# Graph kernel on one core: a second, panel-ordered copy of the transposed adjacency for the panel and search loads

## The chip, the cores and the metric

The kernel runs on one core of a Trainium2 chip. The metric is the device time of one execution in microseconds, as a median of several runs. The profile is of one execution, taken by the hardware profiler. A core has the engines PE (matmul, with its weight loads PEld), DVE, ACT, POOL (GpSimd) and SP, which issues transfers; 16 DMA engines serve the core.

## The reference

Four layers follow each other; each adds to x what it computes from x and one sparse 4096 x 4096 adjacency matrix, and normalizes. N is 4096, D is 256.

```
x = LN(x + adj @ (x * W0))                                    # layer 0
R = (adj + I) / rowsum;  Xf = Xa = x;  Z = 0                  # layer 1
for n in (0, 1):
    A  = top_p_attention(Xa, W1, W2, W3)                      # softmax, smallest set holding 0.9, renormalized
    Xf = R @ Xf;  Xa = A @ Xa
    Z  = Z + Xf @ U1[n].T + Xa @ U2[n].T
x = LN(x + LN(x + Z))
s = x @ Hv                                                    # layer 2: softmax over neighbours
x = LN(x + softmax over j with adj[i,j] != 0 of (adj[i,j] * s[j]) @ x)
edge[i] = sum_j adj[i,j] * adj[j,i]                           # layer 3
x = LN(x + concat(x, adj @ x, edge) @ weight + bias)
```

The density of adj falls with the row and column number: the first tiles of 128 nodes have many neighbours, the last ones few.

## The kernel before

Nodes are cut into 32 tiles of P = 128. The adjacency comes in as `pair`, of shape [4096, 32, 2, 128]: for node j and column tile b, 128 numbers of adj[j] and, right behind them, the same 128 columns of the transposed matrix. Each piece of 128 numbers is 512 bytes, so a load of the transposed part alone reads 512 contiguous bytes at a time. The view `adjT_v` (line 188) names the transposed parts by partition p, row tile t, column tile b.

Two kinds of load read that view, both issued on SP's queue.

- A *panel* (JC = 4 row tiles of one column tile, 256 KB) in `adj_matmul` (line 195) and `all_columns` (line 1392). Eight panels make one target tile I, and 32 matmuls (line 205) add up its row of adj @ x. Panels have a pool of five buffers in layer 0 (`loads=5`) and of four in layers 2 and 3.
- A *half* (HB = 8 blocks of 128 x 128, 512 KB) in `find_columns` (line 472), which only looks for nonzeros. It has two buffers.

In layer 0, a target tile is handled densely or by a list. The first 16 tiles are dense (`dense_0`); the last 16 are listed (`listed_0`): for each of them and each class of source nodes, GpSimd gathers only the rows that have a neighbour in the tile. For that, `seen[p, J, b]` must first hold the largest absolute value of row p of row tile J in column tile b. For the dense tiles it is filled by a reduction of each panel on DVE (line 197); for the others, b from 16 to 31, by `find_columns`, with a reduction of each half (line 473). Between the panels of the first five dense tiles stand all 64 halves: seven row tiles J for each target tile, two halves for each J.

When they are done, `list_columns(1)` builds on DVE and PE the lists of sources for the listed tiles, and writes the index tables idx_x and idx_a (line 357). `gather` (line 380) is GpSimd's indirect transfer with such an index; `pack` gathers adjacency pairs of a listed tile (reading `pair`, both parts) and stores the transposed part as `packed`, blocks of [128, up to 5, 128] in DRAM, which later layers read back as pc (line 418). `listed_steps` gathers the feature rows and multiplies (line 434). `out_0` ends a target tile: layer norm on DVE, projections on PE, stores.

Layer 1 (lines 970 to 1330) computes attention of every node against all, narrowed to candidates, with R through the lists; it reads no panel. In layer 2 the first six target tiles use `all_columns` (48 panels), in layer 3 the first three use `adj_matmul` (24 panels); the others use packed blocks and gathered rows. A fallback, `with_all_columns`, is skipped unless a test of the data fails; it uses panels too.

The order of work on each engine is planned by the tile framework when the kernel is built; only two stretches of layer 1 have an order written out by hand (`manual_schedule`) for PE, ACT, DVE and GpSimd. So in layer 0, panels of later dense tiles stand between the halves of earlier ones.

Of the kernel before, what the change touches and what calls it, by code (L numbers as in the profile page):

```python
# [15 lines left out]
OP = mybir.AluOpType  # L16
AX = mybir.AxisListType

P = 128
# [3 lines left out]
NT = N // P  # L23
# [23 lines left out]
HB = 8  # L47
# [12 lines left out]
LE = P // NL  # L60
# [5 lines left out]
JC = 4  # L66


@with_exitstack
def gnn_kernel(ctx: ExitStack, tc: tile.TileContext, x, pair, W0, W1, W2T, W3T, U1T, U2T,  # L70
               ln_g, ln_b, Hv, W3L, b3, out):
    nc = tc.nc
    PSUM = bass.MemoryType.PSUM
# [50 lines left out]
    for j in range(NT):  # L124
        t = big.tile([P, D + 1], F32, name=f"xw_{j}", tag=f"xa{j}", padded_shape=[P, D + 2])
# [59 lines left out]

    adjT_v = pair.rearrange("(t p) b s i -> p t b s i", p=P)
    pair_r = pair.rearrange("j b s i -> (j b) (s i)")

    def adj_matmul(ps, rhs, I, seen=None, width=D, beside=None, stop=True):

        for c in range(NT // JC):
            a = pools["loads"].tile([P, JC, P], F32, name="panel", tag="panel")
            nc.sync.dma_start(a, adjT_v[:, c * JC:(c + 1) * JC, I, 1])
            if seen is not None:
                nc.vector.tensor_reduce(seen[:, c * JC:(c + 1) * JC, I], a, AX.X, OP.max, apply_absolute_value=True)
            if beside is not None:
                beside(c)
            if callable(rhs):  # L200
                b = rhs(c)
            for k in range(JC):
                j = c * JC + k
                r = b[:, k, :] if callable(rhs) else rhs[j][:, :width]
                nc.tensor.matmul(ps[:, :width], a[:, k, :], r, start=(j == 0), stop=stop and j == NT - 1)  # L205
# [97 lines left out]
    seen = const.tile([P, NT, NT], BF16, name="seen")  # L303
# [163 lines left out]

    def find_columns(J):

        for b in range(LE, NT, HB):  # L470
            t = pools["loads"].tile([P, HB, P], F32, name="half", bufs=2)
            nc.sync.dma_start(t, adjT_v[:, J, b:b + HB, 1])
            nc.vector.tensor_reduce(seen[:, J, b:b + HB], t, AX.X, OP.max, apply_absolute_value=True)

    def out_0(I, ps, sums, xin):
        nc.vector.tensor_scalar_add(rone[:, I:I + 1], sums, 1.0)
# [41 lines left out]
    def dense_0(I):  # L518
        ps = acc_tile("A")
        blocks = list(range(I * NEW, min((I + 1) * NEW, NT)))  # L520
        adj_matmul(ps, XW, I, seen, D + 1, lambda c: [find_columns(J) for J in blocks[c:c + 1]])
        later(out_0(I, ps, ps[:, D:D + 1], XW[I][:, :D]))
# [471 lines left out]
    for k in range(2):  # L994
        t = const.tile([P, N // P + 1], BF16, name=f"ranks_{k}")
# [370 lines left out]
    def nbr_weights(pc, xs, n):  # L1366
        e = pools["gat"].tile([P, PIECE, P], F32, name="pe", tag="pr", bufs=4)
        for k in range(n):
            nc.scalar.activation(e[:, k, :], pc[:, k, :], AF.Exp, scale=xs[k][:, D + 1:])
        nc.vector.scalar_tensor_tensor(e[:, :n, :], pc[:, :n, :], 0.0, e[:, :n, :], op0=OP.not_equal, op1=OP.mult)  # L1370
        return e

    X2 = []
    for I in range(NT):
        t = big.tile([P, D + 2], F32, name=f"x2_{I}", tag=f"xa{I}")
# [13 lines left out]
    def all_columns(ps, I):  # L1389
        for c in range(NT // JC):  # L1390
            a = pools["loads"].tile([P, JC, P], F32, name="panel", tag="panel")
            nc.sync.dma_start(a, adjT_v[:, c * JC:(c + 1) * JC, I, 1])
            xs = X2[c * JC:(c + 1) * JC]
            e = nbr_weights(a, xs, JC)
            for k in range(JC):
                j = c * JC + k
                nc.tensor.matmul(ps[:, :D + 1], e[:, k, :], xs[k][:, :D + 1], start=(j == 0), stop=(j == NT - 1))  # L1397
# [7 lines left out]
    for n, I in enumerate(mixed(HUBS[0])):  # L1405
        ps = acc_tile("A" if n % 2 else "R")
        if I < HUBS[0]:
            all_columns(ps, I)
        else:
            listed_matmul(ps, x2d, D + 1, I, unpack(I), nbr_weights)  # L1410
        rk = one("rk", bufs=3)
        nc.vector.tensor_scalar_max(rk, ps[:, D:D + 1], 1e-37)
        nc.vector.reciprocal(rk, rk)
        out_2(I, ps, rk, X2[I][:, :D], X3[I])
# [17 lines left out]
    for n, I in enumerate(mixed(HUBS[1])):  # L1432
        ps = acc_tile("A" if n % 2 else "R")
        if I < HUBS[1]:
            adj_matmul(ps, X3, I)
        else:
            listed_matmul(ps, x3d, D, I, unpack(I))
        out_3(I, ps, X3[I])
# [38 lines left out]
    def with_all_columns():  # L1477
        U[0], U[1] = load_u(U1T, "w0"), load_u(U2T, "w1")
        for I in range(LE, NT):
            ps = acc_tile("A")  # L1480
            adj_matmul(ps, rows4(x, 1), I, width=D + 1)
            xin = reload(x, I)
            run(out_0(I, ps, ps[:, D:D + 1], xin))
# [55 lines left out]
    leave()  # L1539


_NAMES = ["x", "pair", "W0", "W1", "W2T", "W3T", "U1T", "U2T", "ln_g", "ln_b", "Hv", "W3L", "b3"]


# [21 lines left out]
```

## Time and profile before

| | us |
|---|---|
| median of 3 runs | 2801.77 |
| the runs | 2792.40, 2801.77, 2803.52 |
| the profiled execution, its own time | 2792.35 |
| its span, first to last instruction | 2790.5 |

| engine | busy us | share |
|---|---|---|
| PE | 2248.1 | 81% |
| PEld | 1587.8 | 57% |
| DVE | 2119.5 | 76% |
| ACT | 1510.1 | 54% |
| POOL | 1779.6 | 64% |

Transfers: 354.25 MB in the span. SP's queue (q1) carries 183.10 MB of it and takes 22.5% of the 16 DMA engines' time, GpSimd's (q0) 144.85 MB and 17.7%, ACT's (q10) 23.77 MB and 2.6%. There are 200 panels and 64 halves.

A line of the profile's tables names the kernel's line, the engine, the operation and `out<-in` by the program's names. A wait "A <- B: 56.4, 26, 7.0" says that A's engine stood idle for 56.4 us in 26 waits, the longest 7.0, until B was done. Times are counted from the span's start. The granted clock is the share of full speed that TensorE was allowed.

### The profile page before, as it was taken

The numbers are of one execution on the slowest core, as the hardware profiler recorded it, in microseconds if no ns is written. First come the engines' busy times: TensorE is split into PE (matmuls) and PEld (weight loads), VectorE is DVE, ScalarE is ACT, GpSimd is POOL, SyncE is SP. The second block draws the span as 40 slices with busy tenths as digits, with TensorE's granted clock in tenths as the row PEclk, the third lists the DMA queues.
The fourth block names the chain that finished last, engine by engine and source line by source line (L and its number), as shares of the span: only waits on it lengthen the run. The fifth ranks groups of instructions, "written<-read, shape, count | busy, mean of one in ns | idle before, by whom it ended". The sixth has DMA issues, their size and how long they took to land.

```text
span 2790.5 us, 38070 instructions
## 1 busy us (share of the span) xinstructions
PE 2248.1 (81%) x10712; PEld 1587.8 (57%) x10712; DVE 2119.5 (76%) x6448; ACT 1510.1 (54%) x2428; POOL 1779.6 (64%) x2840
## 2 busy tenths in 40 slices
PE   6768798778888888874778888888888887697997
PEld 4556576345445445442556666666666666475785
DVE  4777566688677777727688999999999996576574
ACT  0001011355566656646688888888888882454111
POOL 1003645356667677765788888888888873775774
PEclk9999899888898989885999999999999998898999
DMA  9996665444445454541211111111111113676664
GB/s 277 275 261 177 200 190 170 134 131 151 123 129 148 136 146 142 147 142 32 65 56 57 54 53 44 55 63 46 45 44 42 41 46 94 207 235 188 196 208 126
DMA packets 354061, 354.25 MB, mean 127 GB/s; under 512 B 35120, under 2 KB 307008, under 8 KB 353840
## 3 DMA queue, kind: packets, MB, share of 16 engines
q1 hardware_dynamic: 272224, 183.10, 22.5%
q0 software_dynamic: 51008, 144.85, 17.7%
q10 hardware_dynamic: 30608, 23.77, 2.6%
q8 instruction: 88, 1.44, 0.2%
q14 instruction: 133, 1.09, 0.1%
HBM read 298.69 MB, written 52.89 MB: 126 GB/s over the span
## 4 chain that ended last, share of the span: by engine, by line
PE 18%; DVE 14%; POOL 9%; ACT 8%; issue 5%; DMA 2%; DVEq 0%; POOLq 0%; ACTq 0%
PE psa L229 4%; PE acc L434 3%; DVE cand L767 3%; PE acc L1397 3%; ACT junk L680 2%; DVE tmp L761 2%; PE pz L874 2%; POOL xg L380 2%; PE lg L570 2%; PE acc L205 1%; ACT junk L686 1%; DVE e L813 1%; ACT e L641 1%; POOL shift L908 1%; ACT junk L644 1%
## 5 line engine op out<-in xcount | busy, mean ns | idle before, releaser
L229 PE MATMUL psa<-v,eT 128*128 128x256 f32 x2048 | 511.3, 397 | 87.7 <-ACT eT L220 87.6
L229 PEld LDWEIGHTS psa<-v,eT 128*128 128x128 f32 x2048 | 399.1, 198 | 168.4 <-ACT eT L220 113.0
L205 PE MATMUL acc<-xw,panel 128*128 128x257 f32 x1024 | 258.8, 408 | 64.1 <-DMA panel<-in_pair 56.7
L380 POOL DMA_INDIRECT xg<-in_x,idx_x x72 | 69.8, 970 | 318.5 <-DVE idx_a L357 237.7
L205 PEld LDWEIGHTS acc<-xw,panel 128*128 128x128 f32 x1024 | 203.2, 204 | 114.9 <-DMA panel<-in_pair 41.5
L680 ACT ACTIVATE junk<-e,h 128x4096 bf16<-128x4096 f32 x64 | 237.4, 3709 | 39.5 <-POOL h L660 24.9
L686 ACT ACTIVATE junk<-e,h 128x4096 bf16<-128x4096 f32 x62 | 230.9, 3724 | 0.1
L380 POOL DMA_INDIRECT xg<-qtab,idx_x x180 | 176.6, 981 | 84.8 <-issue 43.5
L218 PE MATMUL pt<-ident,e 128*128 128x128 f32 x1024 | 159.5, 287 | 83.4 <-DVE e L813 57.3
L380 POOL DMA_INDIRECT g<-tab,idx x160 | 156.9, 981 | 106.2 <-issue 47.4
L380 POOL DMA_INDIRECT xg<-ttab,idx_x x180 | 176.7, 982 | 57.7 <-issue 34.6
L380 POOL DMA_INDIRECT pc<-in_pair,idx_a x180 | 174.0, 967 | 51.9 <-issue 45.5
L218 PEld LDWEIGHTS pt<-ident,e 128*128 128x128 f32 x1024 | 131.7, 148 | 128.3 <-issue 84.6
L767 DVE MAX8 cand<-tmp 128x8 f32<-128x128 f32 x1024 | 203.3, 276 | 1.2
L1022 PE MATMUL lg<-kT,qi 64*128 64x512 f32 x512 | 172.1, 751 | 30.3 <-ACT e L1037 25.0
L1028 DVE MAX8 cand<-e 128x8 f32<-128x256 f32 x512 | 179.1, 412 | 22.8 <-ACT e L1037 21.4
L220 ACT COPY eT<-pt 128x512 f32<-128x512 f32 x256 | 144.9, 591 | 85.3 <-PE pt L218 85.2
L570 PE MATMUL lg<-kT,qi 64*128 64x512 f32 x480 | 140.6, 662 | 55.4 <-ACT junk L644 50.2
L240 ACT COPY xT<-ptx 128x256 f32<-128x256 f32 (+1 forms) x96 | 42.3, 441 | 261.7 <-PE ptx L237 139.2
L380 POOL DMA_INDIRECT xg<-x3d,idx_x x146 | 140.2, 960 | 66.1 <-issue 39.3
L1037 ACT ACTIVATE e<-lg 128x1024 f32<-128x1024 f32 x128 | 130.7, 1021 | 58.5 <-PE lg L1022 58.5
L380 POOL DMA_INDIRECT xg<-x2d,idx_x x126 | 129.4, 1027 | 50.4 <-PE acc L434 19.0
(332 smaller groups left out, 5666.4 us busy)
## 6 DMA issues: line engine op xcount, KB each, us to landing
panel<-in_pair SPq DMA_DIRECT2D x200, 256.0 KB
half<-in_pair SPq DMA_DIRECT2D x64, 512.0 KB
pc<-pk SPq DMA_DIRECT2D x55, 320.0 KB
pc<-pk SPq DMA_DIRECT2D x45, 256.0 KB
tab<-xi ACTq DMA_DIRECT2D x33, 160.0 KB
pc<-pk SPq DMA_DIRECT2D x23, 192.0 KB
x2d<-x SPq DMA_DIRECT2D x32, 129.0 KB
x<-x2d SPq DMA_DIRECT2D x32, 129.0 KB
```

The costliest lines, as they stand in the source:

```text
L205: nc.tensor.matmul(ps[:, :width], a[:, k, :], r, start=(j == 0), stop=stop and j == NT - 1)
L218: nc.tensor.transpose(pt[:, k, :], e[:, (g * 4 + k) * P:][:, :P], ident)
L220: nc.scalar.copy(eT[g], pt)
L229: nc.tensor.matmul(ps[:, :D], eT[g][:, k, :], rhs[j][:, :D], start=(j == 0), stop=stop and j == NT - 1)
L380: nc.gpsimd.indirect_dma_start(out=o, out_offset=None, in_=src, in_offset=bass.IndirectOffsetOnAxis(ap=idx[:, c], axis=0))
L570: nc.tensor.matmul(ps[:, h, :], qi[r, :], kT[r, (n * NC + c) * LC:][:, :LC], start=True, stop=True)
L680: nc.scalar.activation(junk_tile(), e, AF.Relu, bias=h, scale=-1.0, accum_out=part)
L686: nc.scalar.activation(junk_tile(), e, AF.Sign, bias=h, scale=-1.0, accum_out=below)
L767: nc.vector.max(cand[:, c * (NS // 2) + g, :], w[:, g * SEG:(g + 1) * SEG])
L1022: nc.tensor.matmul(lgs[c][:, k, :], qi[r, :], kT[r, c * LC:(c + 1) * LC], start=True, stop=True)
L1028: nc.vector.max(cand[:, b, :], e[:, b * SEG0:(b + 1) * SEG0])
L1037: nc.scalar.activation(both(e, c), lgs.pop(c), AF.Exp, accum_out=sq[:, c:c + 1])
```

## The change

A new input, `panels`, holds the transposed adjacency once more, ordered [32 column tiles, 8 panels, 128 partitions, 4 row tiles, 128]. A panel is then one contiguous piece of 256 KB in which each partition has 2 KB. The loads of panels and of halves read it; gathers still read `pair`. A half is now two panels of one column tile (eight row tiles of one b), where it was eight column tiles of one row tile; the number of halves, their size and their places in the program are the same, and each call of `find_columns(J)` still issues two. The reduction of a half writes eight numbers of `seen` along the row tile instead of along the column tile.

```diff
-def gnn_kernel(ctx: ExitStack, tc: tile.TileContext, x, pair, W0, W1, W2T, W3T, U1T, U2T,
+def gnn_kernel(ctx: ExitStack, tc: tile.TileContext, x, pair, panels, W0, W1, W2T, W3T, U1T, U2T,
...
-    adjT_v = pair.rearrange("(t p) b s i -> p t b s i", p=P)
...
             a = pools["loads"].tile([P, JC, P], F32, name="panel", tag="panel")
-            nc.sync.dma_start(a, adjT_v[:, c * JC:(c + 1) * JC, I, 1])
+            nc.sync.dma_start(a, panels[I, c])
...
     def find_columns(J):
 
-        for b in range(LE, NT, HB):
+        for u in range(2 * J, 2 * J + 2):
+            b, h = LE + u % LE, u // LE
             t = pools["loads"].tile([P, HB, P], F32, name="half", bufs=2)
-            nc.sync.dma_start(t, adjT_v[:, J, b:b + HB, 1])
-            nc.vector.tensor_reduce(seen[:, J, b:b + HB], t, AX.X, OP.max, apply_absolute_value=True)
+            nc.sync.dma_start(t.rearrange("p (c k) i -> p c (k i)", k=JC),
+                              panels[b, h * HB // JC:(h + 1) * HB // JC].rearrange("c p k i -> p c (k i)"))
+            nc.vector.tensor_reduce(seen[:, h * HB:(h + 1) * HB, b], t, AX.X, OP.max, apply_absolute_value=True)
...
     blocks = [a.reshape(N, NT, P) for a in (adj, np.ascontiguousarray(adj.T))]
-    given = [x, np.stack(blocks, axis=2), L0_gnn_W, L1_gnn_W1, np.asarray(L1_gnn_W2).T, np.asarray(L1_gnn_W3).T,
+    panels = blocks[1].reshape(NT // JC, JC, P, NT, P).transpose(3, 0, 2, 1, 4)
+    given = [x, np.stack(blocks, axis=2), panels, L0_gnn_W, L1_gnn_W1, np.asarray(L1_gnn_W2).T, np.asarray(L1_gnn_W3).T,
```

The load in `all_columns` is edited like that of `adj_matmul`.

More of the change, by code (lines that the diff above doesn't have):

```diff
@@ L1391, in all_columns @@
             a = pools["loads"].tile([P, JC, P], F32, name="panel", tag="panel")
-            nc.sync.dma_start(a, adjT_v[:, c * JC:(c + 1) * JC, I, 1])
+            nc.sync.dma_start(a, panels[I, c])
             xs = X2[c * JC:(c + 1) * JC]
@@ L1539, in gnn_kernel @@
     leave()
-_NAMES = ["x", "pair", "W0", "W1", "W2T", "W3T", "U1T", "U2T", "ln_g", "ln_b", "Hv", "W3L", "b3"]
+_NAMES = ["x", "pair", "panels", "W0", "W1", "W2T", "W3T", "U1T", "U2T", "ln_g", "ln_b", "Hv", "W3L", "b3"]
 def kernel(x, adj, L0_gnn_W, L1_gnn_W1, L1_gnn_W2, L1_gnn_W3, L1_gnn_U1, L1_gnn_U2, L1_gnn_ln_g, L1_gnn_ln_b,
```

## The prediction

> **What bounds the kernel now.** I began with the page's slices, because the change touches loads alone and the first question is where loads matter. Each column is 69.8 us.
>
> ```profile
> DMA  9996665444445454541211111111111113676664
> GB/s 277 275 261 177 200 190 170 134 131 151 123 129 148 136 146 142 147 142 32 65 56 57 54 53 44 55 63 46 45 44 42 41 46 94 207 235 188 196 208 126
> ```
>
> Only the first three slices have all 16 DMA engines full, at about 270 GB/s. From slice 19 to 32 (the attention of layer 1) they are nearly idle, and the changed loads don't occur there. Next, the busy table by stretches of time (columns: PE, PEld, DVE, ACT, POOL busy, granted clock, DMA share, GB/s):
>
> ```profile
> 0.00:216.00 216.00, 150.94 (x574) 115.64 (x574) 140.88 (x260) 5.97 (x17) 11.18 (x77) 0.94 1.00 272
> 216.00:246.00 30.00, 29.54 (x169) 21.88 (x168) 29.11 (x84) 7.08 (x25) 0.00 (x0) 1.00 0.51 151
> 246.00:490.00 244.00, 203.24 (x927) 159.10 (x926) 150.10 (x434) 27.91 (x107) 136.28 (x142) 0.91 0.64 185
> ```
>
> Up to 216 us the DMA share is 1.00 while PE is at 70% and DVE at 65%; afterwards PE is at 98% and then 83%, and DMA at 51 and 64%. So 216 us of the span are bound by transfers. The DMA view of 20 to 215 us says of what:
>
> ```profile
> DMA packets 102589, 53.43 MB, mean 274 GB/s; under 512 B 2541, under 2 KB 102577, under 8 KB 102580
> q1 hardware_dynamic: 98041, 49.18, 93.5%
> half<-in_pair SPq DMA_DIRECT2D x60, 512.0 KB
> panel<-in_pair SPq DMA_DIRECT2D x67, 256.0 KB
> ```
>
> SP's queue has 93.5% of the engines' time, and it carries the two loads that are changed. That the stage sets the path is seen in the waits, first those up to 225 us, then one from after it:
>
> ```profile
> PE acc L205 <- DMA panel<-in_pair: 56.4, 26, 7.0
> DVE seen L473 <- DMA half<-in_pair: 55.7, 51, 3.4
> ...
> POOL xg L380 <- DVE idx_a L357: 237.7, 1, 237.7
> ```
>
> PE and DVE each wait 56 us for these loads. GpSimd waits 237.7 us for idx_a, which list_columns(1) writes at 251 us; the timeline has its first operation at 217.0, right behind the last search reduction (215.2 to 216.4). All gathers of the first layer stand behind that. (The chain of waits that the profile follows back breaks off at 1262 us, so it says nothing of this stage.) Later panels are awaited hardly at all: in 2340 to 2580 us "DMA panel<-in_pair: 0.5, 2".
>
> **What the skill says.** "DMA: Bandwidth & Descriptors", Specifications, gives 512 B as the least transfer for line rate. The trace disagrees in part. Its packet records on SP's queue have a median of 27 ns for 512 B, 46 for 1024, 84 for 2048 (the packed blocks pc<-pk) and 102 for 2560: a line with some 8 ns per packet on top, so 512 B gives 19.0 GB/s per engine (303 for 16) and 2 KB 24.4 (390). The same page, "Why small descriptors are slow", names such a fixed cost per packet. Under the section Anatomy of one DMA it gives about 2 us per DMA of fixed time whatever the size. The trace roughly agrees: pairing SP's issues with the queue's completion packets in order, a packed block of 192 KB lands at the earliest 1.94 us after issue, of which 0.5 is data, so 1.45 us is fixed.
>
> **The change, part by part.**
> *Panel and search loads.* Same count (200 and 64), same bytes, same issuing queue, 4 times fewer packets. That contiguous rows become 2 KB packets is shown by pc<-pk: a tile of the same shape, [128, 4, 128], read from contiguous memory, leaves exactly 128 packets of 2048 B each. SP's issue (367 ns in the trace) doesn't depend on the row length in any view; I count it unchanged.
> *Time on the DMA engines in the first stage.* Up to 215 us 64 halves and 75 panels are loaded (8 before 20 us): 53.2 MB, or 103,936 packets of 512 B. At the mean there, 30.1 ns (27 plus 11% for crowding), on 16 engines: 195 us. As 25,984 packets of 2 KB at 84 ns plus the same 11%, 94 ns: 152 us. **That is 43 us of transfer time**; bounds: 84 ns gives 136 us (59 saved), and 107 ns, the mean of the isolated pc<-pk loads, where an engine's first packet takes 200 to 400 ns, gives 174 us (21 saved).
> *What of it becomes time.* Search loads have two buffers, so each buffer runs a loop: issue, landing, its turn on DVE, reduction, next issue. Between 24.2 and 216.4 us there are 61 reductions, so a pair takes 6.3 us. The median landing is 3.9 us after issue, the reduction 1.22, the remaining 1.2 waiting for DVE's or SP's turn. With 2 KB rows the half's own data takes 64 x 30.1 = 1.93 us less 16 x 94 = 1.50, saving 0.43; about one panel that shares the rings saves half of that, 0.21. DVE's turn comes a bit sooner because panels land sooner too: 0.06 to 0.1. I take 0.7 us per pair: **5.6 us instead of 6.3, over 31 pairs 22 us.** The floors are lower: DMA 152 plus some 20 us of other loads is 5.5 us per pair, DVE's own work (141 us in 216) 4.6. So the loop stays the limit and the engines are just below it.
> *Start.* Before 27 us, four halves, eight panels and the x tiles queue up, landings being 7 to 11 us; 4.2 MB at a fifth less time is 3 us.
> *Order of the search.* find_columns takes one column tile and eight row tiles instead of the reverse. The last load is issued in the same place, so the list starts when all have come. DVE's write is 8 elements with a step; the panel reduction already writes with that step, at 685 ns for 512 elements against 1220 for 1024, so I cost it at nothing; had it a price, 0.1 us times 64 is 6 us, in the range.
> *Second half of the first layer.* Everything behind idx_a moves forward. PE was waiting on panels in the first stage, so its share moves too. 53 panels come here, 13.9 MB: 51 us of DMA at 30.1 ns against 40; at a share of 0.64 it is beside other work. The gathers waited for (61 us of DVE's pr behind pc) may gain from it. I take 2 us, bounds 0 and 5.
> *Layers 2 and 3.* 72 panels. Nobody waits for them, PE or ACT covers them. The gathers, which PE does wait for, share the engines at 0.72: 1 us, bounds -5 and 5 (SP's order of loads may shift).
> Host work is not in the time. The gathers of adjacency pairs still read the old array.
> **Sum: 22 + 3 + 3 = 28 us.** From the profiled execution (2792.35, span 2790.5) that is 2764; the median of the runs shown is 9.4 us higher, its lowest 2792.4. I take the middle, 2769.
>
> **Rivals.**
> *The loop was not the limit, transfers were.* With the share at 1.00 the whole 43 us, up to 59, come back and the next limit is DVE. For it: PE and DVE both wait for DMA. Against it: two buffers. It gives 2792 - 48 + 5 = 2749.
> *Hidden.* Landing is mostly fixed latency and DVE's order; the unloaded landing falls only from 3.25 (the least seen) to 2.8, and the time saved in front of the list is spent again on PE, which is at 98 and 83% behind it. Of the 28 us, 6 to 12 are left: 2788, no change. For it: PE's busy 203 of 244 us after the list. Against: PE waits 56 us before it, and that goes too.
> *Slower.* Outside hand-ordered stretches the tile framework plans each engine's order at build time from assumed durations, and this stage is such a one: panel reductions of eight blocks stand between the searches of five. If it takes shorter loads for granted, DVE's queue has searches ahead of panel reductions and layer norm steps. DVE then waits at each for its landing, and panel buffers (five) behind it are not freed, so PE starves. Now DVE waits 55.7 us at 51 of 64 searches. Each further 1 us per search is 64 us; at 0.44 the 28 us are gone, above 0.66 it is slower. At 1 us it is 2797 + 64 - 28 = 2833. Against it: fixed latency is the same, so an order fit for the old loads mostly fits.
> *It doesn't do what it says*, rows staying at 512 B: excluded by pc<-pk as far as I can see.
>
> **How the numbers follow.** A measurement tells 0.5%, 14 us, from no change: faster is below 2788. Main case 0.49 (2755 to 2782), all transfer time 0.17, hidden 0.20, slower 0.12, no shorter packets 0.02. Faster: 0.49 + 0.17 + a fifth of hidden, 0.70. Slower 0.10 (a small part of its case stays within 14 us). Same 0.20. The range 2740 to 2812 leaves out half of the all-transfer case and most of the slower one.
>
> **What would show it.** In the changed profile: 2048 B packets in place of 203,264 of 512 B; in the first three slices about 300 GB/s or more at a share of 0.9; the last search reduction at about 190 us instead of 215; idx_a at 225; waits for half and panel each down by 15 to 25 us; from there on the stages as long as before (244, 772, 1114, 199, 215 us), only earlier. The prediction is wrong if the search reductions end near 215 although packets are 2 KB (loop or order), if they end early but the first layer does not, or if the DVE order between searches has changed.

## The result, and the profile after

The changed kernel takes 2782.41 us (median of 6 runs, 2777.84 to 2786.05) beside 2794.13 us for the kernel before (6 runs). The ratio is 0.9949, 95% interval 0.993 to 0.9968: 12 us or half a per cent, faster. In a later set of runs the pair was measured again: 2782.24 to 2795.36, ratio 0.9954 (0.9939 to 0.997). 28 us were forecast, within a range that holds the result.

The instructions of every engine stand in the same order in both traces, at all 6448 places of DVE and 10,712 of PE, so that each can be compared with its twin. First the slices of the page of the changed kernel (69.6 us each), and its first three stretches (PE, PEld, DVE, ACT, POOL busy, granted clock, DMA share, GB/s):

```profile
DMA  9885665444445445540111111111111113676664
GB/s 285 284 286 162 198 200 160 130 134 136 133 133 147 139 140 146 146 139 31 57 58 57 53 53 49 60 53 46 45 44 42 42 46 97 203 240 188 199 205 124
```
```profile
0.00:206.00 206.00, 149.74 (x572) 113.33 (x573) 139.56 (x260) 5.97 (x17) 11.17 (x77) 0.96 0.88 286
206.00:237.00 31.00, 30.54 (x174) 22.85 (x172) 29.94 (x86) 7.08 (x25) 0.00 (x0) 1.00 0.45 141
237.00:484.00 247.00, 204.40 (x926) 159.23 (x924) 149.70 (x434) 27.89 (x107) 138.11 (x144) 0.90 0.64 185
```

The first stage is 10 us shorter with the same work in it, and the share of the DMA engines' time is down (0.88 for 1.00). They move only 5% more bytes per us (286 for 272 GB/s). The two stretches behind last about as long as before (31 and 247 us for 30 and 244; their borders are set by hand, and the comparison of twins below is finer). The DMA view of 20 to 205 us:

```profile
DMA packets 30756, 53.60 MB, mean 290 GB/s; under 512 B 2571, under 2 KB 6730, under 8 KB 30747
q1 hardware_dynamic: 26028, 49.19, 79.9%
```

For the same 49.2 MB on SP's queue there are 26,028 packets (with the completions) where 98,041 were: the rows are 2 KB. The waits (the first two up to 225 us, the last from 230 to 490 us), then the search reductions and the writes of idx_a by tile, these before and after:

```profile
DVE seen L474 <- DMA half<-in_panels: 47.5, 44, 3.4
PE acc L204 <- DMA panel<-in_panels: 39.3, 23, 4.5
...
POOL xg L379 <- DVE idx_a L356: 229.2, 1, 229.2
```
```profile
L474 DVE TENSOR_REDUCE seen<-half x64: 1207/1226/1228, 6.4 to 205.3; 128x8 bf16<-128x1024 f32 x64
L357 DVE SCALAR_TENSOR_TENSOR idx_a<-free,at x2: 234/326/418, 251.2 to 691.3; 128x80 int32<-128x80 f32 x1, 128x256 int32<-128x256 f32 x1
L356 DVE SCALAR_TENSOR_TENSOR idx_a<-free,at x2: 233/326/418, 241.6 to 686.1; 128x80 int32<-128x80 f32 x1, 128x256 int32<-128x256 f32 x1
```

DVE waits 8 us less for halves and PE 17 less for panels; the last search begins at 205.3 us instead of 215.2, and the list comes 9.6 us sooner (first idx_a at 241.6). From there the engines run mostly 9.5 to 11 us ahead of their twins to the end of the first layer. Between 600 and 2790 us the lead wanders, mostly between 4.5 and 11 us, and ends at 7.5; in the second profile of the same kernel it is 6.7 us at the end of the first layer and 11.2 at the end. The one place of gain that both profiles show is the first 216 us. What comes later goes down in one and up in the other, and I take it for the spread of single executions.

### The profile page after: what moved, and what is told of

Read it like the earlier page. It is cut to its first block, busy times and chain, and to the rows that moved or that the text cites. A ratio compares the mean times of both kernels' runs of the same rounds, so it can differ in the third digit from the quotient of the medians.

```text
span 2784.2 us, 38070 instructions
## 1 busy us (share of the span) xinstructions
PE 2246.9 (81%) x10712; PEld 1586.1 (57%) x10712; DVE 2117.0 (76%) x6448; ACT 1511.1 (54%) x2428; POOL 1780.3 (64%) x2840
## 3 DMA queue, kind: packets, MB, share of 16 engines
q14 instruction: 133, 1.09, 0.1%
## 4 chain that ended last, share of the span: by engine, by line
DVE 16%; PE 15%; POOL 9%; ACT 7%; issue 5%; DMA 2%; DVEq 0%; POOLq 0%; ACTq 0%; SPq 0%
DVE cand L768 4%; PE psa L228 3%; PE acc L433 3%; PE acc L1398 3%; DVE tmp L762 3%; ACT junk L681 2%; PE pz L875 2%; POOL xg L379 2%; DVE top L745 1%; DVE rest L747 1%; PE lg L571 1%; POOL shift L909 1%; ACT junk L687 1%; ACT e L642 1%; POOL rs L925 1%
## 5 line engine op out<-in xcount | busy, mean ns | idle before, releaser
L681 ACT ACTIVATE junk<-e,h 128x4096 bf16<-128x4096 f32 x64 | 237.4, 3709 | 43.4 <-POOL h L661 28.3
```

What stands on the lines that cost most here:

```text
L681: nc.scalar.activation(junk_tile(), e, AF.Relu, bias=h, scale=-1.0, accum_out=part)
```

## The experiments

Each time is compared with the kernel before in the same set of runs. From the traces I worked out four quantities for each kernel: the end of the last search, the first write of idx_a, PE's idle time ahead of that and after it, and the end of the last listed matmul (line 434 before) of the first layer. That end is PE's work plus its two idle times by the way they are counted, so the sum proves nothing; what it tells is which of the three has changed.

| kernel | total, ratio to before | last search | idx_a | PE idle ahead, after | layer 0 ends (PE) |
|---|---|---|---|---|---|
| before | | 216.4 | 251.2 | 65.6, 46.3 | 508.4 |
| changed, first profile | 0.9949 | 206.6 | 241.6 | 56.7, 44.1 | 498.2 |
| changed, second | 0.9954 | 209.8 | 244.5 | 58.0, 45.0 | 502.1 |
| panels only | 1.0001 | 216.5 | 251.3 | 64.8, 43.4 | 508.0 |
| halves only | 0.9987 | 216.3 | 252.1 | 66.1, 43.1 | 510.4 |
| changed, 3 half buffers | 0.9970 | 168.8 | 208.1 | 63.2, 42.6 | 504.9 |
| before, 3 half buffers | 1.0018 | 181.2 | 221.8 | 71.2, 42.8 | 516.8 |
| changed, halves by GpSimd | 1.0057 | 251.4 | 283.0 | 82.3, 51.0 | 539.9 |
| before, halves by GpSimd | 1.0134 | 265.7 | 298.1 | 95.0, 54.4 | 561.3 |
| changed, 8 panel buffers | 0.9964 | 206.9 | 242.0 | 57.6, 48.2 | 500.4 |

**Panels alone.** Only the two panel loads read the new array; `find_columns` is that of before.

> Panels read the new layout, the searches read the old one. The planned order of every engine is that of the kernel before. Theory A (the search loop: two half buffers, each waiting for its own landing, set the pace of the first stage, and panels only share the rings): the searches end 0 to 3 us earlier than 216.4, total -2 us (0 to -4). Theory B (the first stage is bound by the DMA engines' total time, so that each shortened byte counts alike): panels are 19.7 of the 53.2 MB, so 37% of the change's -12 us: searches end 4 us earlier, total -4.5 us. Half landing: A 3.8 to 3.9 us, B 3.8.

Measured 2794.63 us to 2794.75, ratio 1.0001 (0.9987 to 1.0016). The table of 0 to 200 us, for the kernel before and then for this one, and its search reductions:

```profile
0.00:200.00 200.00, 138.60 (x520) 105.81 (x521) 128.79 (x243) 5.97 (x17) 11.18 (x77) 0.93 0.99 271
0.00:200.00 200.00, 138.34 (x526) 104.31 (x526) 128.21 (x243) 5.98 (x17) 11.25 (x77) 0.93 0.90 273
L473 DVE TENSOR_REDUCE seen<-half x64: 1199/1220/1222, 7.8 to 215.3; 128x8 bf16<-128x1024 f32 x64
```

The engines' share has gone from 0.99 in the kernel before to 0.90, at 273 GB/s after 271, and the last search hasn't moved (216.5). So a tenth of the DMA engines' time was freed and nothing came of it: **a share of 1.00 was not the bound.** That speaks against theory B. Theory A gave 0 to 3 us at the searches and 0 to 4 in total, which fits.

**Halves alone.** `find_columns` is that of the change, panels are read from the old array.

> The searches read the new layout, panels the old one; order as before. Theory A: nearly the whole gain of the change: searches end 8 to 10 us earlier than 216.4, total -10 us. Theory B: 63% of it: searches end 6 us earlier, total -7.5 us. Both: packets on SP's queue in the first stage are part 512 B and part 2 KB, DMA share near 0.93.

Measured 2789.06 us to 2794.75, ratio 0.9987 (0.9971 to 1.0003).

```profile
0.00:200.00 200.00, 140.08 (x526) 105.81 (x526) 128.51 (x244) 5.98 (x17) 11.18 (x77) 0.92 0.89 272
```

Again the share falls, by nearly as much as with both parts (0.88), and the searches don't end sooner in the profiled execution. It took 2800.11 us to a median of 2789.06, so it can't show where the gain of its set, about 4 us, would come from. Both theories missed: A wanted nearly the whole gain from halves, B most of it. The two parts alone give 0 and about -4 us, together -13: the sum of the parts is less than the whole, by 9 us where the three intervals together leave some 7.5 (an estimate: their half widths of 4 to 4.5 us, added as squares). So it is likely, and not certain. Panels and halves follow each other in one queue, but that this is why was not shown.

**Three half buffers, new and old layout.** `name="half", bufs=3` in each kernel.

> The changed kernel with three half buffers instead of two. The planner then puts only 36 panels (not 66) ahead of the last search, the same order as in the old-layout kernel with three buffers. Theory A: with a third buffer landing is covered, and the stage runs at the speed of transfers (33.5 MB of halves and 10 MB of panels and 4 MB of x at 330 to 390 GB/s, 125 to 145 us) or DVE (64 x 1.23 + 36 x 0.69 + ends, about 120 us): last search at 140 to 155 us, and 25 to 35 us earlier than in the old layout with three buffers. Theory C (it is DVE's order, not landing): last search at 165 us or later and within 10 us of the old layout with three buffers. Total: PE has 30 panels more (about 55 us of its work) behind the list, and it is at 83 to 98% there, so the end moves less than the searches: A -10 to -30 us against the changed kernel, C within 8 us of it.

> The kernel before with three half buffers (old layout): the other corner of the square. Theory A and B: the DMA engines were already full (share 1.00), so transfers set the pace: 47 MB at 270 to 290 GB/s plus the start, last search at 165 to 180 us because 30 panels now come later; total 0 to -15 us against before. Theory C: as the other three-buffer kernel, within 10 us. The layout's worth with three buffers, this against the changed kernel with three: A 20 us or more, C 8 us or less.

Measured 2786.42 us (ratio 0.9970, 0.9956 to 0.9983) and 2798.74 us (1.0018, 1.0006 to 1.0031). The first write of idx_a, new layout and then old:

```profile
L356 DVE SCALAR_TENSOR_TENSOR idx_a<-free,at x2: 233/326/418, 208.1 to 692.2; 128x80 int32<-128x80 f32 x1, 128x256 int32<-128x256 f32 x1
```
```profile
L357 DVE SCALAR_TENSOR_TENSOR idx_a<-free,at x2: 235/326/417, 221.8 to 701.8; 128x80 int32<-128x80 f32 x1, 128x256 int32<-128x256 f32 x1
```

The stretch from 24 us to the last search, for old and new layout with two buffers, then for old and new with three:

```profile
24.00:215.00 191.00, 141.27 (x553) 109.63 (x553) 135.44 (x252) 5.97 (x17) 0.00 (x0) 0.93 1.00 273
24.00:205.00 181.00, 136.43 (x544) 105.70 (x544) 132.41 (x247) 5.97 (x17) 0.00 (x0) 0.95 0.87 288
24.00:180.00 156.00, 102.55 (x320) 71.37 (x318) 107.48 (x173) 5.99 (x17) 0.00 (x0) 0.80 1.08 287
24.00:167.00 143.00, 96.97 (x317) 69.48 (x318) 106.09 (x172) 5.98 (x17) 0.00 (x0) 0.80 0.91 311
```

Three things follow. The layout is worth 12.4 us at the last search and 12.3 in total, as with two buffers, and not the 25 to 35 of theory A. C's 10 us are exceeded too, but its other values hold: the last search at 165 or later (168.8), and a total within 8 us of the changed kernel (by the ratios 4 to 6 us slower). The old layout with three buffers was forecast no slower than before, and is 4 us slower.

A third buffer raises the bytes per us by 5% in the old layout and 8% in the new. In the old one the share goes to 1.08 with it (the share sums up the packets' times, which can overlap): a share of 1.00 was no ceiling. Two buffers held the stage back, then, but not by much. Most of the sooner list comes from 30 panels fewer ahead of it, 7.9 MB or some 29 us at 273 GB/s (an estimate).

And a list that is ready 33 us sooner than in the changed kernel (43 than in the kernel before) brings nothing by itself: the first layer ends at 504.9, behind the changed kernel. PE's work is the same (399 us after 397), and its idle time ahead of the list is 63 instead of 57 us; only 36 panels, not 66, feed PE ahead of the last search, which fits.

**The changed kernel again, and the searches on GpSimd's queue.** In the latter pair `find_columns` issues with `nc.gpsimd.dma_start`, in the new layout and in the old.

> The changed kernel once more, timed beside the others of this set. All theories: 8 to 15 us faster than before; in the profile idx_a within 3 us of 241.6, PE idle ahead of it 54 to 59 us, last listed matmul of the first layer near 498. If the change and halves alone (-4 us) and panels alone (0) add up, it would be only 4 us faster; I expect more than the sum, since a search load still stands behind panels in one queue.

> The changed kernel with the search loads issued on GpSimd's queue (idle until the list is made), so that SP's queue holds only panels there. The planner then puts 85 panels ahead of the last search. Theory P (the first layer ends when PE has done its work; what counts is PE's idle time ahead of the list, not when the list is ready): panels no longer stand behind search loads, PE idle ahead of the list falls from 56 to 25 to 45 us, and the layer ends 10 to 25 us earlier than in the changed kernel although idx_a comes no earlier than 241 (more panels ahead of it); total -10 to -20 us against the changed kernel. Theory L (what counts is when idx_a is ready, as the prediction had it): idx_a at 245 to 265, total 0 to +20 us against the changed kernel.

> The kernel before (old layout) with the search loads on GpSimd's queue; the same planned order as the changed kernel with that queue. If rows of 512 B cost by filling the DMA engines, transfers set the pace here too (share 1.00, 57 MB by 220 us): idx_a 15 to 30 us later than in the new layout with this queue, PE idle ahead of the list 15 to 25 us more, total 12 to 25 us more. If the engines' time did not matter, the two are within 5 us.

The changed kernel repeats its gain (13 us). The new layout with GpSimd's queue takes 2813.73 us (ratio 1.0057, 1.0036 to 1.0077), the old one 2830.69 (1.0134, 1.0106 to 1.0162). The layout is worth 17 us there, and idx_a comes 15 us sooner; both are what was expected if the transfers' time counts, and more than the 5 us if it doesn't. But the share that went with this, 1.00 in the old layout, was 0.88: transfers cost time there without full engines. The first of the two kernels was forecast wrongly by both theories. Its first 200 us, its stretch of 180 to 260 us, and PE's longest wait in that stretch:

```profile
0.00:200.00 200.00, 151.67 (x580) 120.26 (x581) 125.41 (x251) 5.98 (x17) 47.59 (x128) 0.86 0.83 260
180.00:260.00 80.00, 44.33 (x211) 36.91 (x209) 52.28 (x100) 0.37 (x1) 13.55 (x19) 0.78 0.64 203
PE psl L322 <- DVE tmp L319: 20.9, 1, 20.9
```

PE does get more done in the first 200 us (580 matmuls to 553). But the last searches stand behind 85 panels, and from 180 to 260 us PE is busy 44 of 80 us. PE's own part of the list (psl, line 322) stands in its order behind 640 of the 1024 matmuls of dense tiles. It reaches it at 233 us and waits 20.9 us, until after the last search (251.4), with the other dense work behind it; in the kernels with two buffers on SP's queue this step waits for nothing. So a late list costs where PE's order meets it, and an early one does not help. PE's idle time ahead of the list is 24 us more than in the repeat of the changed kernel, after it 6, its work 8, and the layer ends 38 us later, the kernel 31.

**Eight panel buffers.** `enter(loads=8, ...)` for the first layer.

> The changed kernel with eight panel buffers in the first layer instead of five; the searches stand between the same panels as before. If PE's buffers hold SP's queue up (in the kernel before SP waited 17 us for PE's matmuls there), panels and searches start earlier: last search 5 to 10 us earlier than 206.6, PE idle ahead of the list 5 to 10 us less, total -5 to -10 us. If the two half buffers hold it up, as the waits of SP for halves and their reductions (64 us) say: within 3 us of the changed kernel in all three.

Measured 2785.43 us to 2795.36, ratio 0.9964 (0.9949 to 0.9979), last search 206.9, PE idle 57.6. From the waits of SP's own queue up to 225 us:

```profile
SPq L472 <- DMA half<-in_panels: 35.3, 41, 2.4
SPq L472 <- DVE seen L474: 28.6, 24, 1.7
SPq L194 <- PE acc L204: 16.2, 14, 4.7
```

SP waits 64 us for halves and their reductions and 16 for PE, as with five buffers (17.1): panel buffers hold nothing up, as the second of the two cases had it.

**Half the bytes, new and old layout.** A search loads one panel (256 KB) in place of two and reduces it twice through a repeated view, in buffers of the old size. It leaves out half of the rows. The edit in the new layout:

```diff
-            nc.sync.dma_start(t..., panels[b, h * HB // JC:(h + 1) * HB // JC]...)
+            nc.sync.dma_start(t, panels[b, 2 * h + 1])
-            nc.vector.tensor_reduce(seen[:, h * HB:(h + 1) * HB, b], t, ...)
+            nc.vector.tensor_reduce(seen[...].rearrange("p (c k) -> p c k", k=JC),
+                                    t.unsqueeze(1).to_broadcast([P, HB // JC, JC, P]), ...)
```

> The changed kernel with searches that load one panel (256 KB) instead of two and reduce it twice, so that DVE's work stays and the moved bytes are halved; the search leaves out half of the rows, so the lists lack neighbours. 67 panels stand ahead of the last search, as 66 did. In the two earlier profiles of the changed kernel a search landed 3.76 and 3.88 us after issue, where the prediction's working (0.43 us saved on its own data, 0.21 on the panel ahead) gave 3.3. Theory D (landing is data time on the rings plus a fixed part): half the data takes 0.75 us off, landing 2.9 to 3.2, a buffer's loop 5.1 instead of 5.8 to 5.9, last search 180 to 190 us. Theory F (landing is mostly latency of the first packets and of the slowest engine, whatever the bytes): landing 3.4 or more, last search 197 us or later.

> The kernel before (rows of 512 B) with searches that load 256 KB instead of 512 and reduce them twice; half of the search is left out, the lists lack neighbours and the fallback runs behind, so only the first stage counts (up to the last search). Planned order as in the new-layout kernel with half the bytes, where a search landed 2.79 us after issue and the last one ended at 177.0 us. Theory G (transfers move 2 KB rows no faster than 512 B rows once the slowest of 16 engines is waited for: the long packets eat the saving): landing 2.8 to 2.95, last search 176 to 184. Theory H (the rows' worth grows when data is a smaller part): landing 3.1 or more, last search 188 us or later. By the packet times alone (8 x 94 ns against 32 x 30) landing would be 0.21 us longer than with 2 KB, 3.0, and the last search 7 us later.

In both the lists lack neighbours and the fallback ran behind (22,782 and 22,762 us in all), so only the first stage is read. The search reductions, new layout and then old:

```profile
L473 DVE TENSOR_REDUCE seen<-half x64: 1209/1226/1228, 5.5 to 175.8; 128x8 bf16<-128x1024 f32 x64
```
```profile
L473 DVE TENSOR_REDUCE seen<-half x64: 1203/1220/1223, 5.7 to 181.1; 128x8 bf16<-128x1024 f32 x64
```

The last searches end at 177.0 and 182.4 us. A buffer's loop can be split into the landing of each search (issue to the last of its 16 completions), its turn on DVE, the reduction and the next issue. The means of searches 9 to 64, in us (a landing's mean has a standard error of 0.04 to 0.08; that the sum agrees with the loop only shows that no term was left out):

| kernel | landing | turn on DVE | reduction | to next issue | sum | loop measured |
|---|---|---|---|---|---|---|
| before | 3.97 | 0.86 | 1.22 | 0.03 | 6.08 | 6.12 |
| changed | 3.76 | 0.78 | 1.23 | 0.03 | 5.80 | 5.81 |
| changed, second | 3.88 | 0.78 | 1.23 | 0.04 | 5.93 | 5.92 |
| panels only | 3.92 | 0.97 | 1.22 | 0.03 | 6.14 | 6.18 |
| halves only | 3.99 | 0.80 | 1.23 | 0.03 | 6.05 | 6.09 |
| old, half the bytes | 2.96 | 0.67 | 1.22 | 0.14 | 4.99 | 4.99 |
| new, half the bytes | 2.79 | 0.65 | 1.23 | 0.22 | 4.89 | 4.87 |

Halving the bytes takes 1.0 us off in both layouts (3.97 to 2.96; 3.76 and 3.88 to 2.79). The loop falls with it, by 1.1 and 0.9 to 1.0 us, at the same work of DVE and nearly the same order, which DVE's order alone (theory C) would not do. So bytes count, as theory D said, and theory F falls; but **256 KB cost the same 1 us whether the rows are 512 B or 2 KB.** The new layout takes only 0.1 to 0.2 us off a landing, at either size. That is near G at the full size; at half the size the 0.17 us agree with the packet times (0.21). The two kernels with half the bytes ran on two other chips than those with the full size, one profile each. The fall of 1 us is far beyond the standard errors; a difference of 0.1 to 0.2 between layouts is 1 to 3 of them, and is less sure.

**Runs of 4 KB.** A third copy of the transposed adjacency in which a search has one run of 4 KB per partition; panels stay.

> The changed kernel with one more copy of the transposed adjacency in which a search is contiguous, so that each partition reads one run of 4 KB instead of two of 2 KB; the planned order is unchanged. If the cost per packet were what remains: 8 packets of 4 KB per engine at 159 ns against 16 of 2 KB at 84 save 0.07 us per search, nothing to see (within 3 us of 207 for the last search, total within 4 us of the changed kernel). If run length still mattered[...]: last search 5 us earlier or more. If the long packets (one in twenty over 119 ns) come once per transfer and engine, their share grows from one in 16 to one in 8 and landing stays at 3.7 to 3.9 us.

3107.06 us to 3112.97, ratio 0.9972 (0.9953 to 0.999): faster than the kernel before, and no gain over 2 KB rows can be seen beside 0.9949 and 0.9954. This chip took 3113 us for the kernel before. The search landing is 3.79 us, between the two profiles of the changed kernel, as the third case had it; the last search is at 216.4, DVE's turn taking 1.03, where the cases that named a value had 210 or less. There is no profile of the changed kernel from this chip, so that miss is not explained.

**Searches cut in two.** 128 loads of 256 KB in four buffers.

> The changed kernel with the searches cut in two: 128 loads of 256 KB in four buffers, which take the same room as two of 512. The planner puts only 36 panels ahead of the last search, as with three buffers of 512 KB. If the first layer's end is PE's work plus its idle time, an earlier list is worth nothing by itself: last search at 155 to 172, idx_a at 195 to 212, PE idle ahead of the list 55 to 65 us, last listed matmul 498 to 508, total within 6 us of the changed kernel. If the list's time counted, it would be 20 to 35 us faster than the changed kernel.

3080.45 us to 3072.25, ratio 1.0023 (1.0003 to 1.0044), on another slower chip. idx_a at 217.0, 25 to 28 us sooner than in the changed kernel, and PE idle ahead of it 70.3 us. The kernel is slower than the one before, some 20 us slower than the changed one by the ratios, and the last listed matmul ends at 528.5. What I had written for "an early list is worth nothing" is missed too: by 5 us at the last search, at idx_a and at PE's idle time, and by some 15 to 20 at the layer's end and in total. All lie on the side away from the other theory, which had the kernel 20 to 35 us faster. How much of it is this chip's, which has longer stretches with gathers, was not separated.

## Why the prediction was right, and where it was not

**Direction and place: right.** The loads of the first stage give the gain, the packets are 2 KB, the stages behind keep their length, the panels of layers 2 and 3 and the strided write of `seen` give nothing to be seen (a reduction is 1226 ns after 1220).

**The loop as the limit: right in the main.** The loop follows the landing (1.0 us less of it with half the bytes takes 0.9 to 1.1 off the loop), eight panel buffers change nothing, and the rival in which all the transfer time comes back (2749) is out, since freed engine time was left idle (0.88). With three buffers the rate rose by 5 and 8% only, so the two buffers are not the whole of the limit.

**The size: wrong in one term.** "The half's own data takes 64 x 30.1 = 1.93 us less 16 x 94 = 1.50, saving 0.43; about one panel that shares the rings saves half of that, 0.21." The landing fell by 0.1 to 0.2 us, not 0.64, and the loop by 0.2 to 0.3, not 0.7. Over 31 pairs that is 6 to 10 us in place of 22, which is what the searches gained. Split by what stands ahead in SP's queue, the 23 searches behind another search land 3.70 us after issue before and 3.65 and 3.73 in the two profiles after: the 0.43 of the half's own data are not there. The 33 behind a panel land at 4.16 before and at 3.85 and 3.99 after, and at 4.11 with either part alone. The start gave 1.4 to 1.7 of its 3 us (the third reduction ends at 25.4 us, then at 23.7 and 24.0), the stages behind none of theirs that can be seen.

The term that failed is the 94 ns for a packet of 2 KB. From the halved bytes, 8 packets per engine less take 0.97 to 1.09 us off, 121 to 136 ns each, and for rows of 512 B the 32 packets 1.01, 31.6 ns each: the same time per byte. In the packet records of the changed kernel (20 to 200 us) a 2 KB packet has a median of 84 ns, but a mean of 98, 5% are over 119 and 1% over 518; of the 512 B packets of before, 1% are over 41. The long ones come with the searches: the 2 KB packets have a mean of 88 where panels alone have them, and of 103 where halves alone do. A search has 256 such packets on 16 engines; with packets taken in the order of the queue, its last one ends 3.57 us after issue (median of searches 9 to 64), no sooner than before, 3.49. That long packets make an engine late, and with it the search, fits this and is argued, not tried. The bound of 107 ns, which the prediction had from isolated loads, was nearer than the value that it took.

The range held because it was wide; the result lies at the end of the main case (2755 to 2782), nearer to *hidden* (2788) than to the 2769 that was forecast. Most of the signs named for the main case failed by the same term: the last search at 206.6 instead of 190, idx_a at 241.6 instead of 225, the first slices at 285 GB/s instead of 300, the wait for halves 8 us shorter instead of 15 to 25. (Of the 203,264 packets of 512 B, 167,936 belong to the changed loads; the others stay.)

"The DMA share is 1.00 ... So 216 us of the span are bound by transfers" was half right. The stage waits for the landing of transfers; the engines' share was no sign of a bound, as panels alone (0.90, no time gained) and three buffers in the old layout (1.08, more bytes per us) show.

"Everything behind idx_a moves forward": it did, by as much as idx_a itself, but an earlier idx_a alone does not bring that. With three buffers idx_a moved forward by 33 us more and the end did not. In the first profile of the changed kernel, PE's idle time ahead of the list is down 8.9 us (65.6 to 56.7) with the layer's end down 10.2; the idle time after it (2.2 less) and the work (0.7 more) hardly move. The prediction had named this ("PE was waiting on panels in the first stage, so its share moves too") without seeing that it was the one that counts. Only where PE reaches its own step of the list before the searches are done, as with GpSimd's queue, does the list hold PE up.

**The rivals.** *Slower*, by a changed order on DVE: the order did not change with the layout at all. Where the order did change, by a third buffer or another queue, it moved the list by more (33 us sooner, 41 later) than the layout did (7 to 10). *Hidden* came nearest in size (6 to 12 us left of 28), but not by its mechanism: what was missing had not been saved in the first place, rather than spent on PE behind the list.

Left open: why panels alone and halves alone give less than the two together, why a search's own 2 KB rows save nothing in its landing, and what holds the rate at 311 GB/s with three buffers. No version tried beats the changed kernel.

## What to carry to other kernels

A DMA share of 1.00 shows that engines hold packets, not that they set the time (here a tenth of it could be freed for nothing, and 1.08 was reached). Where a loop over few buffers stands beside it, write down the loop (landing, turn, use, next issue) and ask what the change takes off each term. Price a longer row by what a load's last completion gains, not by the median packet. And before counting an earlier result as time saved, sum up the busy and idle time of the engine that ends the stage.

## What was unexpected of the hardware

Rows of 2 KB moved a 512 KB load in no less time per byte than rows of 512 B, as far as its landing tells (1.0 us per 256 KB in both), though their median packets differ (84 ns to 4 x 27). Chips differed by more than any change tried here that leaves the work whole: the kernel before took 2794 to 2795 us in three sets of runs, and 3113 and 3072 on two other chips. In the profile from the first of these (the kernel with runs of 4 KB) the first stage is 7 us longer than in the repeat of the changed kernel, the attention of layer 1 (1262 to 2376 us) some 9, and the stretches with gathers, 246 to 1262 and 2376 to the end, 180 and 140.
